# Macaron block on one core: group sums on GpSimd, ScalarE in program order in the attention, a written order for the first four tiles, and a base product behind the last gating

## The chip, the cores and the metric

The kernel runs on one core of one Trainium2 chip. The core has TensorE (PE in the profile; its weight loads are listed as PEld), VectorE (DVE), ScalarE (ACT), GpSimd (POOL) and SyncE (SP), which issues all the DMAs here. The metric is the device time of one launch in microseconds, lower is better. All data are 32-bit floats.

## The reference

Four sequences of 256 tokens, 512 features: 1024 tokens in all. The block is a feed-forward layer at half weight, attention, and the same feed-forward layer again:

```python
x = x + 0.5 * ffn(layernorm(x))
x = x + attn(layernorm(x))          # 32 query heads, 8 key/value heads of 128, rope,
                                    # softmax over a sliding window of 128 tokens, then @ wo
x = x + 0.5 * ffn(layernorm(x))

def ffn(xf):                        # 8 experts of rank 16, the best two of each token
    probs = softmax(xf @ W_router.T)
    w = top2(probs), divided by their sum
    h = einsum("td,erd->ter", xf, lora_A)
    return xf @ W_base.T + b_base + einsum("ter,eor,te->to", h, lora_B, w) * 2.0
```

The normalisations have no learned scale. Both feed-forward layers use the same weights, and each subtracts and divides per token before anything is multiplied.

## The kernel before

**Data.** The 1024 tokens are eight tiles `xt[0]` to `xt[7]` of 128 tokens (`x` in the profile), which stay in SBUF from the first load to the last store; tiles 0 to 3 are the first half, 4 to 7 the second. A half has two batches (sequences) of two tiles. The loads are issued on SP in this order: tiles 0 and 1, the narrow weights `ar_sb` (expert A matrices and router side by side, 136 columns), tiles 2 and 3, the base weights `wb_sb`, the bias, tiles 4 to 7, and then the attention weights.

**Feed-forward (`ffn`, L264 to 317)** is cut into steps named by a letter and a tile number, and strings such as "A0 M2 N2" give their order:
- M (`measure`, L198): on VectorE the statistics `st` (L200) and mean with variance `mv` (L202), on ScalarE the square root `sd` (L204).
- N (`norm`, L207): on VectorE the reciprocal `rs`, in the first layer (`f1`) also the shift `sh`; then the normalised tile `xc`, on ScalarE in `f1` and on VectorE in the others; four transposes on TensorE into one PSUM bank `pt` (L222) and a copy on ScalarE to `xn` (L223). M runs within N if it was not asked for before.
- A (`narrow`, L281): the product with the narrow weights, `pa` (L287), copied by ScalarE to `hl` (L291); GpSimd adds the bias to the tile (L292).
- R (`route`, L226 to 261): the top two of eight experts for all tiles of the step. That is a row of small VectorE operations, one exponential on ScalarE (L241), and the gating of `hl` by its shares on GpSimd (L261).
- B (`base`, L297): the base product `po` (L300), which stays open in its PSUM bank.
- G (`gated`, L302): the gated `hl` transposed on TensorE (L306) and copied to `ht` by ScalarE (L308).
- L (`leave`, L310): the last matmul into `po` (L312), then x + 0.5 po on VectorE (L313), then what follows for that tile: in `f1` the attention's normalisation of the tile before it, in the second layer (`f2`) the store.

**Attention.** The work is cut into units (half, group, batch): 2 halves, 8 key/value groups of 4 query heads, 2 batches, so 32 units with the half outermost; unit (1,7,1) is the last. For a unit:
- `scores` (L451): `sa` and `sb` on TensorE (L460, L473). VectorE adds the mask and takes the maxima `mx`. Queries of the first 128 tokens of a sequence attend within them; for the later ones two blocks of 64 keys are chosen.
- `exponentials` (L484): eight exponentials of 128x128 on ScalarE (L490), with their sums, and their reciprocal on VectorE (L494).
- `normalize` (L496): two products of 128x512 on GpSimd (L499).
- `transposes` (L503): eight transposes on TensorE. ScalarE copies one bank to `p0` (L508), VectorE masks the other twice into `p1` (L516, `p` in the profile).
- `values` (L522): two banks, `oa` (L527) and `ob` (L531). ScalarE copies each to `oT` (L528, L532). The copy of `ob` is what the output products wait for.
- `outputs` (L538): four groups of output products (`y`, L555), seven half-size products in place of eight by Strassen's scheme (in Winograd's form). The operand sums `oTs` are four GpSimd operations (`sums_a`, L114). The first group needs no sum, the second the second of them, the last two the others too. For a batch, the parts that belong to both tiles are gathered over the eight groups of a half in `z16` and `z75` (L564; at group 0 by a ScalarE copy, L560).
- `add_sums` (L571): after a half's last group, six additions a batch of `z` and `x` that finish the scheme, on VectorE (L581). For the first half it is queued in `late` behind the outputs of units (0,7,0) and (0,7,1), so it runs within the unit that follows each. For the second half both batches' sums run in unit (1,7,1), since group (1,7) of batch 1 takes plain products (`out_project`, L583 to 590) instead.

Between these run the projections of later groups: `keys` (`pp_k`, L351), `project_v` (`pv`, L444, copied by ScalarE at L448) and `queries` (L377, seven products again, with `u` and `v` as VectorE's temporary sums at L395, and `rope` at L333 to 346, whose last additions are GpSimd's). Their operand sums are `wqs` (L114) for the query weights, made two groups ahead in units with b = 1, and `wos` (L119) for the output weights, made in the group's own unit with b = 0, both on GpSimd.

**What sets the order.** The program is written in Tile, which schedules each engine's instructions by its own estimate of when they are ready, except for the engines named in `tc.manual_schedule`, which keep the order of the program. Before the attention, PE and DVE are in program order, but only for the first four tiles (L623). From the first unit on (L656), GpSimd alone is. Tile pools limit how far work may run ahead: PSUM has four banks with tag "mm" (products) and four with tag "s" (transposes, scores, `pa`); `wq`, `wqs`, `wos`, `ht` and `xs` have one buffer, `xc` three, `oT` four (it also holds `xn`).

The first layer's normalisation of four tiles and the first part of their products follow the string in L624, then the two halves' steps are interleaved (L626 to 631). The second layer for the first half is split by batches into eight pieces each ("N0", "N1 A0", ... "L1"), put into `loose` when its `add_sums` is queued, and taken from it in the last three units (L685 to 691): five pieces and one in unit (1,6,1), the same in (1,7,0), the last four in (1,7,1). The second layer for the second half follows the last unit, in the order of the list at L714, mixed with the last output projection (`None`).

Of the kernel before, what the change touches and what calls it, by code (L numbers as in the profile page):

```python
# [14 lines left out]
ALU = mybir.AluOpType  # L15
# [3 lines left out]
B, S, D = 4, 256, 512  # L19
T = B * S  # L20
NT = T // P
NH, NKV, HD = 32, 8, 128
G = NH // NKV
E, R = 8, 16
# [13 lines left out]
def macaron_kernel(  # L38
# [165 lines left out]
        nc.scalar.activation(std, mv[:, 1:2], AF.Sqrt, bias=eps)  # L204
        moments[tag, t] = mv, std

    def norm(t, xn, i, tag):  # L207
        if (tag, t) not in moments:
            measure(t, tag)
        mv, std = moments[tag, t]  # L210
        rstd = sb.tile([P, 1], F32, tag="rstd", bufs=4, name=f"rs_{tag}_{t}")
        nc.vector.reciprocal(rstd, std)
        xc = sb.tile([P, D], F32, tag="xc", bufs=3, name=f"xc_{tag}_{t}")
        if tag == "f1":
            shift = sb.tile([P, 1], F32, tag="shift", bufs=4, name=f"sh_{tag}_{t}")
            nc.vector.scalar_tensor_tensor(shift, mv[:, 0:1], -1.0, rstd, ALU.mult, ALU.mult)
            nc.scalar.activation(xc, xt[t], AF.Identity, bias=shift, scale=rstd)
        else:
            nc.vector.tensor_scalar(xc, xt[t], mv[:, 0:1], rstd, ALU.subtract, ALU.mult)
        pt = ps.tile([P, KC, P], F32, tag="s", bufs=4, name=f"pt_{tag}_{t}")  # L220
        for c in range(KC):
            nc.tensor.transpose(pt[:, c, :], xc[:, ts(c, P)], ident)  # L222
        nc.scalar.copy(xn[:, :, ts(i, P)], pt)  # L223
# [40 lines left out]
    def ffn(tiles, tag, then):  # L264
        n, t0 = len(tiles), tiles[0]
        xf, po, state = {}, {}, {}

        def x_of(i, c):
            return xf[i // 2][:, c, ts(i % 2, P)]

        def enter(i):
            if i % 2 == 0:
                xf[i // 2] = sb.tile(
                    [P, KC, 2 * P], F32, tag="oT", bufs=4, name=f"xn_{tag}_{tiles[i]}"
                )
            norm(tiles[i], xf[i // 2], i % 2, tag)

        def look(i):
            measure(tiles[i], tag)

        def narrow(i):  # L281
            t = tiles[i]
            if i == 0:
                state["hl"] = sb.tile([P, TPH, E * R + E], F32, tag="hl", name=f"hl_{tag}_{t0}")[:, :n, :]
            pa = score_bank(f"pa_{tag}_{t}")
            for c in range(KC):
                nc.tensor.matmul(  # L287
                    pa[:, : E * R + E], x_of(i, c), ar_sb[:, c, :],
                    start=(c == 0), stop=(c == KC - 1),
                )  # L290
            nc.scalar.copy(state["hl"][:, i, :], pa[:, : E * R + E])  # L291
            nc.gpsimd.tensor_tensor(xt[t], xt[t], half_bias, ALU.add)  # L292

        def shares():
            route(t0, n, state["hl"], tag)

        def base(i):  # L297
            po[i] = mm_bank(f"po_{tag}_{tiles[i]}")
            for c in range(KC):
                nc.tensor.matmul(po[i], x_of(i, c), wb_sb[:, c, :], start=(c == 0), stop=False)  # L300

        def gated():  # L302
            hl = state["hl"]
            pt = ps.tile([P, n, P], F32, tag="s", bufs=4, name=f"ph_{tag}_{t0}")
            for i in range(n):
                nc.tensor.transpose(pt[:, i, :], hl[:, i, : E * R], ident)  # L306
            state["ht"] = sb.tile([P, TPH, P], F32, tag="ht", bufs=1, name=f"ht_{tag}_{t0}")
            nc.scalar.copy(state["ht"][:, :n, :], pt)  # L308

        def leave(i):  # L310
            out, t = po.pop(i), tiles[i]
            nc.tensor.matmul(out, state["ht"][:, i, :], lb_sb, start=False, stop=True)  # L312
            nc.vector.scalar_tensor_tensor(xt[t], out, 0.5, xt[t], ALU.mult, ALU.add)  # L313
            then(t)

        steps = {"M": look, "N": enter, "A": narrow, "B": base, "L": leave, "R": shares, "G": gated}
        return lambda s: steps[s[0]](*(int(i) for i in s[1:]))


# [251 lines left out]
    def add_sums(h, b):  # L571
# [5 lines left out]
        for dst, other in (  # L577
            (z16[:, hi], z16[:, lo]), (x0, z16), (x0[:, hi], z75[:, hi]),
            (z75[:, lo], z16[:, hi]), (z75[:, hi], z75[:, lo]), (x1, z75),
        ):  # L580
            nc.vector.tensor_tensor(dst, dst, other, ALU.add)  # L581

    def out_project(h, g, b, i, oT):  # L583
        t = h * TPH + 2 * b + i
# [35 lines left out]


    halves = [ffn(tiles(h, 0, BPH), "f1", norm_later) for h in range(NHALF)]
    with tc.manual_schedule(engines={mybir.EngineType.PE, mybir.EngineType.DVE}):  # L623
        for step in "M0 M1 N0 N1 A0 M2 N2 A1 M3 N3 B0 A2 B1 A3".split():  # L624
            halves[0](step)
    for h, order in (  # L626
        (0, "R B2"), (1, "N0 N1"), (0, "B3 G"), (1, "A0"),
# [25 lines left out]
            queue.popleft()()  # L653

    last = units[-1]
    ctx.enter_context(tc.manual_schedule(engines={mybir.EngineType.Pool}))  # L656
    ahead = scores(*units[0])
    exponentials(*ahead)
    for u, (h, g, b) in enumerate(units):
# [34 lines left out]
        if left > 1:  # L694
            ahead = scores(*units[u + 1])
        else:
            f2 = [ffn(tiles(h, b, 1), "f2", store) for b in range(BPH)]
            f2[0]("N0")
            f2[0]("N1")
        oT = values(h, g, b, p0, p1)  # L700
        if left > 1:
            exponentials(*ahead)
# [9 lines left out]
                for n in ("N0", "N1 A0", "A1 R", "B0", "B1", "G", "L0", "L1")  # L712
            )
    for n, order in (  # L714
        (0, "A0 A1 R"), (None, 0), (0, "B0"), (None, 1), (1, "N0"), (0, "B1"), (1, "N1 A0 A1 R"),
        (0, "G L0 L1"), (1, "B0 B1 G L0 L1"),
    ):
        if n is None:
            out_project(*last, order, oT)
# [49 lines left out]
```

## Time and profile before

| | |
|---|---|
| time, median of 3 runs | 805.71 us (805.61 to 806.04) |
| time of the profiled execution | 806.56 us |
| its span, first to last instruction | 804.9 us |
| TensorE busy | 784.5 us, 97% |
| VectorE busy | 496.1 us, 62% |
| GpSimd busy | 462.0 us, 57% |
| ScalarE busy | 223.1 us, 28% |
| mean granted TensorE clock | 0.996 |
| DMA, mean | 61 GB/s |

The span is that of one profiled execution; the time is what the device took for a launch, so it is somewhat longer than its span. Rows of the profile name the engine, the line, the operation and the program's names with buffer numbers left out (`xc_f` is an `xc` of a feed-forward layer, `xc_a` one of the attention). The bracket behind a row is the time its engine stood idle before it, and what ended that. "Granted clock" is the share of full speed that TensorE was given. In the page's forty slices it is 1.0 or 0.9 in tenths nearly everywhere; one slice near the end shows 8. Times within the execution are counted from the start of the span: the first transposes start at 6.45 us, and the last matmul ends at 801.04.

### The profile page before, as it was taken

To read this page: it belongs to the slowest core of one execution; us is meant where nothing else is said; L and a number is where in the kernel's file an instruction comes from. 1 tells how busy PE (TensorE), PEld (TensorE's weight loads), DVE (VectorE), ACT (ScalarE), POOL (GpSimd) and SP (SyncE) were. 2 spreads that over 40 slices of the span, in tenths; PEclk is the share of its full clock that TensorE was granted. 3 is DMA by queue.
4 is the path that set the end of the run, shared out by engine and by line. 5 is a ranking of instruction groups with operands and counts; after the bars stand their busy time and mean duration, and the time that the engine had idled before them with its cause. 6 is when DMAs were issued, how large, how long until landed. Compare 5 with 4: busy or idle time off the path is not lost.

```text
span 804.9 us, 10161 instructions
## 1 busy us (share of the span) xinstructions
PE 784.5 (97%) x3524; PEld 604.4 (75%) x3524; DVE 496.1 (62%) x1222; ACT 223.1 (28%) x761; POOL 462.0 (57%) x520
## 2 busy tenths in 40 slices
PE   5999999999999999999999999999999999999897
PEld 4557878787878787887878787878787877867553
DVE  3458573738384847467689737483848474757553
ACT  5242333222222221314033332222222213123231
POOL 5412875766757474748475757666574747456221
PEclk9999999999999999999999999999999999999899
DMA  8400121212120203130221112121202020100001
GB/s 295 149 1 23 70 66 53 91 53 66 53 85 37 89 1 105 40 105 13 73 73 53 65 53 92 52 67 53 66 33 85 2 104 1 53 1 26 1 27 53
DMA packets 33556, 48.91 MB, mean 61 GB/s; under 512 B 1248, under 2 KB 14304, under 8 KB 33504
## 3 DMA queue, kind: packets, MB, share of 16 engines
q1 hardware_dynamic: 33504, 48.26, 17.8%
q8 instruction: 28, 0.46, 0.2%
q14 instruction: 24, 0.20, 0.1%
HBM read 46.15 MB, written 2.10 MB: 60 GB/s over the span
## 4 chain that ended last, share of the span: by engine, by line
PE 89%; DVE 6%; ACT 2%; POOL 1%; issue 1%; DMA 1%; SPq 0%; DVEq 0%; ACTq 0%
PE q L377 23%; PE y L555 22%; PE pp_k L351 7%; PE po_f L300 6%; PE pv L444 6%; PE ob L531 6%; PE sb L473 4%; PE sa L460 3%; PE oa L527 3%; PE pa_f L287 2%; PE po_f L312 2%; PE t L512 2%; PE t L507 2%; ACT pr L490 1%; PE y L587 1%; DVE z L581 1%
## 5 line engine op out<-in xcount | busy, mean ns | idle before, releaser
L344 POOL TENSOR_TENSOR qT<-ra_q,rb_q 128x256 f32<-128x256 f32 x64 | 46.6, 728 | 154.2 <-DVE rb_q L335 154.2
L555 PE MATMUL y<-wo,oT 128*128 128x256 f32 x368 | 95.7, 383 | 0.0
L335 DVE TENSOR_TENSOR rb_q<-q,sin_sb 64x512 f32<-64x512 f32 x128 | 88.1, 688 | 1.7
L114 POOL TENSOR_TENSOR oTs<-oT 128x256 f32<-128x256 f32 x62 | 45.6, 735 | 57.8 <-ACT oT L532 55.4
L555 PEld LDWEIGHTS y<-wo,oT 128*128 128x128 f32 x368 | 71.0, 193 | 10.0
L508 ACT COPY p<-t 128x512 f32<-128x512 f32 x32 | 18.8, 587 | 193.3 <-PE t L507 193.3
L564 DVE TENSOR_TENSOR z<-y,z 128x512 f32<-128x512 f32 x54 | 37.2, 689 | 54.4 <-PE y L555 54.4
L499 POOL TENSOR_TENSOR pr<-pr,sm 128x512 f32<-128x512 f32 x64 | 66.3, 1058 | 2.9 <-DVE sm L494 2.9
L555 PE MATMUL y<-wos,oTs 128*128 128x256 f32 x248 | 65.0, 385 | 0.9 <-POOL oTs L114 0.8
L490 ACT ACTIVATE pr<-pr,nm 128x128 f32<-128x128 f32 x128 | 50.0, 392 | 44.4 <-DVE nm L487 31.8
L444 PEld LDWEIGHTS pv<-wv,xa 128*128 128x128 f32 x256 | 48.6, 190 | 18.1 <-issue 12.9
L377 PE MATMUL q<-xa,wq 128*128 128x256 f32 x256 | 60.8, 379 | 0.0
L377 PE MATMUL q<-xs,wqs 128*128 128x256 f32 x256 | 60.6, 379 | 0.0
L377 PE MATMUL q<-xs,wq 128*128 128x256 f32 x256 | 60.5, 379 | 0.0
L531 PE MATMUL ob<-p,v 128*128 128x512 f32 x128 | 60.5, 593 | 0.0
L444 PE MATMUL pv<-wv,xa 128*128 128x256 f32 x256 | 60.0, 379 | 0.0
L351 PE MATMUL pp_k<-xa,wk 128*128 128x512 f32 x128 | 57.6, 593 | 0.3 <-DVE rb_q L335 0.3
L300 PE MATMUL po_f<-wb_sb,xn_f 128*128 128x512 f32 x128 | 57.7, 593 | 0.0
L564 DVE TENSOR_TENSOR x<-y,x 128x256 f32<-128x256 f32 (+1 forms) x62 | 33.8, 545 | 37.9 <-PE y L555 37.8
L555 PEld LDWEIGHTS y<-wos,oTs 128*128 128x128 f32 x248 | 47.3, 192 | 9.0 <-POOL oTs L114 2.5
L377 PEld LDWEIGHTS q<-xa,wq 128*128 128x128 f32 x256 | 48.5, 190 | 6.9 <-DVE mv_a L202 0.2
L377 PEld LDWEIGHTS q<-xs,wqs 128*128 128x128 f32 x256 | 48.6, 190 | 6.6
(138 smaller groups left out, 1546.8 us busy)
## 6 DMA issues: line engine op xcount, KB each, us to landing
wq<-in_wq_dram SPq DMA_DIRECT2D x16, 1024.0 KB, 5.5
wo<-in_wo_dram SPq DMA_DIRECT2D x16, 1024.0 KB, 5.0
wk<-in_wk_dram SPq DMA_DIRECT2D x16, 256.0 KB, 2.5
wv<-in_wv_dram SPq DMA_DIRECT2D x8, 512.0 KB, 3.5
x<-in_x_dram SPq DMA_DIRECT2D x8, 256.0 KB, 7.0
out_dram<-x SPq DMA_DIRECT2D x8, 256.0 KB, 2.0
wb_sb<-in_w_base_dram SPq DMA_DIRECT2D x1, 1024.0 KB, 8.0
ar_sb<-in_w_ar_dram SPq DMA_DIRECT2D x1, 272.0 KB, 5.2
```

The source lines that it names most:

```text
L114: nc.gpsimd.tensor_tensor(dst, p, q, op)
L300: nc.tensor.matmul(po[i], x_of(i, c), wb_sb[:, c, :], start=(c == 0), stop=False)
L335: nc.vector.tensor_tensor(twice(b[o : o + half, :]), twice(src[i : i + half, :]), angle(sin_sb[o : o + half, :]), ALU.mult,)
L344: nc.gpsimd.tensor_tensor(old_q, a[:, :, 0, :], b[:, :, 0, :], ALU.add)
L351: nc.tensor.matmul(pp, w[:, c, :], xa[h][:, c, :], start=(c == 0), stop=(c == KC - 1))
L377: nc.tensor.matmul(bank[:, ts(j, S)], w[:, c, ts(j, HD)], x[:, c, :], start=(new and j == 0 and c == 0), stop=(c == 1), skip_group_check=True,
L444: nc.tensor.matmul(pv[:, : 2 * HD], xa[h][:, c, ts(i, P)], weights["v", h, g][:, c, :], start=(c == 0), stop=(c == KC - 1),)
L490: nc.scalar.activation(pr[:, n, :], src, AF.Exp, bias=nm[:, n : n + 1], scale=scale, accum_out=sm[:, n : n + 1],)
L499: nc.gpsimd.tensor_tensor(w, w, sm[:, n : n + G].unsqueeze(2).to_broadcast([P, G, P]), ALU.mult)
L531: nc.tensor.matmul(po, v[:, 2 * b + n, cols], p1[n], start=(n == 0), stop=(n == 1))
L555: nc.tensor.matmul(py[:, ts(i, D // 2)], lhs[n - 1][:, c, :], weights["os", h, g][n - 1][:, c, :], start=(i == 0 and c == 0), stop=(c == 1 ...
L564: nc.vector.tensor_tensor(dst, py[:, : len(which) * D // 2], dst, ALU.add)
```

## The change

1. `norm` is split: `scale` makes `xc`, and `norm` transposes it. New steps are X (`scale` alone) and T (`norm` of a tile already scaled). The string for the first four tiles is new, and ScalarE is put in program order there too: tiles 0 and 1 are transposed and copied before tile 2 is scaled.
2. From the attention's first unit to the end, ScalarE keeps the program order, as GpSimd does.
3. The six additions of `add_sums` go from VectorE to GpSimd, where they stand in program order: in the units behind (0,7,0) and (0,7,1) between the normalisation (L499) and the weight sums, and in unit (1,7,1), for both batches, behind its normalisation.
4. In the last unit, "N0 N1" of the second layer's tiles 4 and 5 (in `f2[0]`) is placed behind `values` instead of ahead of it.
5. In the list for the last four tiles, the last base product B1 goes behind the last gating G.

```diff
--- before.py
+++ after.py
@@ -204,7 +204,7 @@
         nc.scalar.activation(std, mv[:, 1:2], AF.Sqrt, bias=eps)
         moments[tag, t] = mv, std
 
-    def norm(t, xn, i, tag):
+    def scale(t, tag):
         if (tag, t) not in moments:
             measure(t, tag)
         mv, std = moments[tag, t]
@@ -217,6 +217,12 @@
             nc.scalar.activation(xc, xt[t], AF.Identity, bias=shift, scale=rstd)
         else:
             nc.vector.tensor_scalar(xc, xt[t], mv[:, 0:1], rstd, ALU.subtract, ALU.mult)
+        moments[tag, t] = xc
+
+    def norm(t, xn, i, tag, scaled=False):
+        if not scaled:
+            scale(t, tag)
+        xc = moments[tag, t]
         pt = ps.tile([P, KC, P], F32, tag="s", bufs=4, name=f"pt_{tag}_{t}")
         for c in range(KC):
             nc.tensor.transpose(pt[:, c, :], xc[:, ts(c, P)], ident)
@@ -268,15 +274,21 @@
         def x_of(i, c):
             return xf[i // 2][:, c, ts(i % 2, P)]
 
-        def enter(i):
+        def enter(i, scaled=False):
             if i % 2 == 0:
                 xf[i // 2] = sb.tile(
                     [P, KC, 2 * P], F32, tag="oT", bufs=4, name=f"xn_{tag}_{tiles[i]}"
                 )
-            norm(tiles[i], xf[i // 2], i % 2, tag)
+            norm(tiles[i], xf[i // 2], i % 2, tag, scaled)
 
         def look(i):
             measure(tiles[i], tag)
+
+        def shape(i):
+            scale(tiles[i], tag)
+
+        def turn(i):
+            enter(i, scaled=True)
 
         def narrow(i):
             t = tiles[i]
@@ -313,7 +325,7 @@
             nc.vector.scalar_tensor_tensor(xt[t], out, 0.5, xt[t], ALU.mult, ALU.add)
             then(t)
 
-        steps = {"M": look, "N": enter, "A": narrow, "B": base, "L": leave, "R": shares, "G": gated}
+        steps = {"M": look, "X": shape, "T": turn, "N": enter, "A": narrow, "B": base, "L": leave, "R": shares, "G": gated}
         return lambda s: steps[s[0]](*(int(i) for i in s[1:]))
 
 
@@ -578,7 +590,7 @@
             (z16[:, hi], z16[:, lo]), (x0, z16), (x0[:, hi], z75[:, hi]),
             (z75[:, lo], z16[:, hi]), (z75[:, hi], z75[:, lo]), (x1, z75),
         ):
-            nc.vector.tensor_tensor(dst, dst, other, ALU.add)
+            nc.gpsimd.tensor_tensor(dst, dst, other, ALU.add)
 
     def out_project(h, g, b, i, oT):
         t = h * TPH + 2 * b + i
@@ -620,8 +632,10 @@
 
 
     halves = [ffn(tiles(h, 0, BPH), "f1", norm_later) for h in range(NHALF)]
-    with tc.manual_schedule(engines={mybir.EngineType.PE, mybir.EngineType.DVE}):
-        for step in "M0 M1 N0 N1 A0 M2 N2 A1 M3 N3 B0 A2 B1 A3".split():
+    with tc.manual_schedule(engines={
+        mybir.EngineType.PE, mybir.EngineType.DVE, mybir.EngineType.Activation
+    }):
+        for step in "M0 M1 X0 X1 T0 T1 M2 A0 X2 M3 A1 T2 X3 B0 T3 A2 B1 A3".split():
             halves[0](step)
     for h, order in (
         (0, "R B2"), (1, "N0 N1"), (0, "B3 G"), (1, "A0"),
@@ -653,7 +667,7 @@
             queue.popleft()()
 
     last = units[-1]
-    ctx.enter_context(tc.manual_schedule(engines={mybir.EngineType.Pool}))
+    ctx.enter_context(tc.manual_schedule(engines={mybir.EngineType.Pool, mybir.EngineType.Activation}))
     ahead = scores(*units[0])
     exponentials(*ahead)
     for u, (h, g, b) in enumerate(units):
@@ -695,8 +709,6 @@
             ahead = scores(*units[u + 1])
         else:
             f2 = [ffn(tiles(h, b, 1), "f2", store) for b in range(BPH)]
-            f2[0]("N0")
-            f2[0]("N1")
         oT = values(h, g, b, p0, p1)
         if left > 1:
             exponentials(*ahead)
@@ -712,8 +724,8 @@
                 for n in ("N0", "N1 A0", "A1 R", "B0", "B1", "G", "L0", "L1")
             )
     for n, order in (
-        (0, "A0 A1 R"), (None, 0), (0, "B0"), (None, 1), (1, "N0"), (0, "B1"), (1, "N1 A0 A1 R"),
-        (0, "G L0 L1"), (1, "B0 B1 G L0 L1"),
+        (0, "N0 N1 A0 A1 R"), (None, 0), (0, "B0"), (None, 1), (1, "N0"), (0, "B1"), (1, "N1 A0 A1 R"),
+        (0, "G L0 L1"), (1, "B0 G B1 L0 L1"),
     ):
         if n is None:
             out_project(*last, order, oT)
```

The scheduler answers to these. In the instruction lists of the changed program TensorE's first steps are the transposes of tiles 0 and 1, `pa` 0, `pa` 1, the transpose of tile 2, `po` 0, the transpose of tile 3, `pa` 2. VectorE has the statistics of tile 4 ahead of the `mv` of tile 3. The square roots of the first half's second layer, and what follows them, move from the time of the first sums to the end of the kernel. The order of the loads and stores on SP is as before.

## The prediction

> **What bounds the kernel now.** I read the page first (busy shares, the forty slices, the chain that ended last), then the waits, then the timeline in every place where TensorE idles.
>
> ```profile
> PE 784.5 (97%) x3524; PEld 604.4 (75%) x3524; DVE 496.1 (62%) x1222; ACT 223.1 (28%) x761; POOL 462.0 (57%) x520
> ...
> PE 89%; DVE 6%; ACT 2%; POOL 1%; issue 1%; DMA 1%; SPq 0%; DVEq 0%; ACTq 0%
> ```
>
> TensorE is busy 97% of the span and carries 89% of the chain. The change adds no matmul, so it can win only TensorE's idle time and any stretch at half clock; everything else is hidden while TensorE has a next matmul. Idle times of TensorE over 0.2 us in the timeline: 6.45 and 2.50 at the start; 0.42 at 381; 1.09 at 437; 0.28 at 448; 0.68 and 0.42 at 677 to 680; 3.21 at 749; 0.52 at 799; three of 0.24. The three large places:
>
> ```profile
> 10.27 0.57 ACT L223 COPY xn_f<-pt_f 128x512 f32<-128x512 f32 x1
> ...
> 10.89 2.18 PE L287 MATMUL pa_f<-ar_sb,xn_f 128*128 128x136 f32 x8 [2.50 <-ACT xn_f L223]
> ...
> 13.58 0.69 DVE L200 BATCH_NORM_STATS2 st_f<-x 128x6 f32<-128x512 f32 x1 [2.83 <-DMA x<-in_x_dram]
> ...
> 410.82 2.04 POOL L499 TENSOR_TENSOR pr<-pr,sm 128x512 f32<-128x512 f32 x2
> ...
> 412.82 1.45 POOL L114 TENSOR_TENSOR wqs<-wq 128x512 f32<-128x512 f32 x1
> ...
> 417.48 1.34 POOL L114 TENSOR_TENSOR wqs<-wq,wqs 128x512 f32<-128x512 f32 x1
> ...
> 421.58 0.72 POOL L114 TENSOR_TENSOR oTs<-oT 128x256 f32<-128x256 f32 x1 [2.76 <-ACT oT L532]
> ...
> 424.17 1.03 PE L555 MATMUL y<-wos,oTs 128*128 128x256 f32 x4
> ...
> 438.37 1.99 PE L377 MATMUL q<-xa,wqs 128*128 128x256 f32 x8 [1.09 <-DVE v L395]
> ...
> 740.09 1.65 DVE L581 TENSOR_TENSOR x<-x,z 128x512 f32<-128x512 f32 x1
> ...
> 748.98 0.40 ACT L490 ACTIVATE pr<-pr,nm 128x128 f32<-128x128 f32 x1 [5.78 <-DVE nm L486]
> ...
> 752.32 2.08 PE L555 MATMUL y<-wos,oT 128*128 128x256 f32 x4 [3.21 <-ACT oT L532]
> ```
>
> A row is start, duration, engine, line, tiles; the bracket is the idle time before it and what ended it. Front: the first transposed tile waits in ScalarE's queue until 10.27, behind tile 2. Middle: GpSimd has only 2.76 us of slack before the `oTs` sums, and TensorE takes them at 424.17 the moment they are there. Tail: VectorE's last group sums (L581) and the routing push the scores back, ScalarE starts its exponentials at 748.98, and `oT` comes behind five of them.
>
> ```profile
> core 0: us, PE busy (x) PEld busy (x) DVE busy (x) ACT busy (x) POOL busy (x), PEclk, DMA share, GB/s
> ...
> 754.90:758.30 3.40, 3.40 (x9) 2.68 (x9) 0.45 (x1) 0.00 (x0) 2.58 (x3) 0.50 0.00 0
> ```
>
> The table by stretch: TensorE is full, at granted clock 0.50, as from 751.5 on. The seven `y` groups take 9.26 us from 752.32, against 6.04 in the chain for other units: the wait at 749 costs 3.2 twice.
>
> **Front.** Splitting the normalisation in two adds no instruction; it moves them. ScalarE now copies tiles 0 and 1 (0.57 each) right after their transposes, at 7.5 and 8.5, so both `pa` products (2.18 each at the early half rate, as at 10.89) run from 8.4 to 12.7 at worst. But `hl` of tile 0 (to 10.9) stands ahead of `xc` of tile 2 (0.81, now to 11.8, was 10.06), and VectorE's order now puts the statistics of tile 4 ahead of `mv` of tile 3. Tile 4 lands at 13.58, and behind it wait `mv` 3 (to 14.5), its `sd` (14.8), `rs`, and `sh`, which ends near 15.85 behind a 1.24 us GpSimd op as the `sh` issued at 15.21 did; then ScalarE: `sd` 4, `xn` 2 (0.57), `xc` 3 to 17.06. So the transpose of tile 3 starts at 17.1 (was 14.90). What follows it, up to the third base product, is 0.44 + 0.93 + 3.43 + 0.93 = 5.7: it starts at 22.9 to 23.1, was 24.06. **-1.0**; bounds -2.0 and +0.3.
>
> **ScalarE in order in the attention.** The copy of `ob` goes ahead of the eight exponentials instead of behind three. At 378 it starts 0.75 earlier and the 0.42 wait at 381 goes: **-0.4**. At 677 `ob` itself ends at 677.2, the copy cannot be earlier, and 0.68 + 0.42 stay. Elsewhere a `pv` product stands between and covers it. The exponentials start up to 0.6 later; their normalisation is needed ten us later, after the queries, so that costs nothing.
>
> **Group sums on GpSimd, middle.** Per call four adds of 128x256 and two of 128x512. Nearest rows of the same engine: `oTs` 0.73 at a pitch of 0.805, `wqs` 1.27 at 1.35. GpSimd goes in program order, so the sums stand between L499 (to 412.82) and `wqs`. They wait twice for products: z16 412.85, x0 at 414.15 (its product is added until 414.08), x0's second half at 415.87, then 416.67, 417.47, 418.27 to 419.54. Behind them are four `wqs` (5.4) to 424.95 (before: 418.8), then `oTs`. Its third op, which the product of 424.17 needs, ends at 424.95 + 2 x 0.805 + 0.73 = 427.3. TensorE has meanwhile done the two groups that need no sum, to 424.0, and idles **3.3**. What comes back: VectorE no longer jams, so the 1.09 and 0.28 go, and about 0.3 of issue and of the `ob` wait. The second call ends at 436.3; the statistics that wait for it on VectorE hold `u` and `v` until 438.6, but TensorE wants `v` only at 440.3: 1.7 of cover, and past it TensorE would wait one for one. `wos` moves from 433.9 to 441.7, wanted after 451. SP's loads follow TensorE's reads and shift with it. Net **+1.5**; bounds +0.5 and +3.
>
> **Clock.** Does that 3.3 us idle halve the clock? The row says a wait of 3.21, with only 0.66 us of transposes around its start, did, for 6.8 us. The Trainium skill ("TensorE: Matmul & The Clock Gate", What's actually happening) says that the clock falls after at least one idle window of about 3.4 us, in windows that run freely. By the rule 3.3 does not fill a window, and the loss is 0; by the row it costs (6.8 - 1) / 2 = 2.9. The trace agrees with the window (6.8 is two of them) but fell after less than a whole one. The same page (Part 4) has transposes not counted as busy; then the idle stretch there was 748.33 to 752.32, 4.0, longer than mine. So I take no fall as likelier, 2.9 as the upper end.
>
> **Tail.** The normalisation of the first half's four tiles moves here from the middle: two more table loads on ScalarE net. The row has 1.28 (425.73), the skill ("ScalarE: Activation LUTs", What ACT_TABLE_LOAD costs) 2.66 with a drain; at 425.73 the square root follows at 427.03, so I use 1.28; by the rule two of these chains would be 1.4 later each, +2.8. Step by step:
> - 711.92: exponentials end 708.8, load and `sd` to 710.44, `xc` (0.55 alone, 1.6 beside GpSimd) by 711.9. The second `sd` queues behind `xn`, so the tiles go one by one: 0.7 idle instead of 0.48. +0.25.
> - 729: `oTs` is wanted one bias product (0.86) earlier than before: 0.6 idle (was 0.1), +0.4.
> - 736: again one by one, +0.2.
> - 740 to 750: without L581's 1.4 to 1.65 VectorE finishes the maxima at 749.2 or earlier, and the copy of `ob` no longer waits for exponentials: `ob` ends 749.1, copy to 749.85, `y` at 749.9, 0.7 idle before its sums, so `y` ends at 756.6. Before: 761.4. **-4.8** with the three lines above in it; the half clock is gone.
> - GpSimd's twelve sums now start after the last normalisation (756.45); x of tile 5 is complete at 762.3. VectorE's statistics wait for it, and behind them are two L313 and the masked `p`: the first `ob` goes at 765.55 instead of 763.8, **+1.75**, 0.3 more at `oa`.
> - The first `pt` of the last two tiles was under other work; now `xn` behind it is waited for, **+0.7** (and ScalarE's load before its `sd` ends at 769.25, covered by the out projection). The base product behind the last gating covers the copy that cost 0.52, **-0.5**: the gated shares are ready on GpSimd near 791.9 and wanted at 792.5.
> Sum -4.8 + 1.75 + 0.3 + 0.7 - 0.5: tail **-2.6**. Of the two loads, by the skill's figure, +2.8 more, which would eat it. Bounds -4.5 and +0.3.
>
> **Sum.** -1.0 - 0.4 + 1.5 - 2.6 = -2.5. The two ends added up, -6.4 and +3.2, do not come together; taken as independent they reach 2.4 below the forecast and 3.5 above (root of the squares), and half of each is what I allow the forecast itself. The profiled execution's own time is 806.56 (span 804.9, 1.66 around it), 0.85 above the median of 805.71. I take the difference off the median: **803.2**.
>
> **The rivals.**
> - *The half clock moves to the middle.* The idle stretch at 424 meets a free-running window badly: +2.9, 806.1, no change. For: the row at 749. Against: the rule and the missing transposes. 0.28.
> - *Slower: the sums are too dear for GpSimd.* One mechanism: they stand ahead of `oTs` in the middle and ahead of the statistics in the tail, so each us that six of them need over 5.5 costs about one at 424 and one at 765. With a longer stall the clock falls too (+2.9). It decides from 6.1 us for the six, since -2.5 + 2.9 + 2 x 0.6 = +1.6. For: L114 beside L581 took 1.45 and 1.61 for 1.27; at that rate 6.9 us, -2.5 + 2.9 + 2.8 = +3.2, 808.9. Against: after the move VectorE reads a PSUM operand in those stretches, beside which L114 stays at 1.27. 0.16.
> - *The front does not do what its order says*, tile 4 setting the pace as before: +1.0 on the forecast, 804.2; it lies in the forecast's own range, 802.0 to 804.9.
>
> **How the numbers follow.** Forecast 0.57 (the front rival 0.08 of it), half clock 0.27, dear sums 0.16. About 0.2% (1.6 us) can be told from no change: faster is below 804.1, slower above 807.3. Faster: the forecast without its front rival, 0.49. Same: that 0.08 and 0.22 of the half clock, 0.30. Slower: 0.05 of the half clock and the dear sums, 0.21. The range 801.6 to 807.8 leaves out 0.06 below and 0.14 above.
>
> **What would show it.** Right: `pa` from 8.4 and the third transpose near 17; one TensorE wait of 3.3 on POOL `oTs` near 423, none on `v`; no wait of 3.2 on ACT `oT` and clock 1.00 near 750; a wait of 1.7 on DVE `p` near 763. Wrong: clock 0.50 after the middle wait; sums over 0.85 and 1.4 each; a tail that ends within 1 us of the old one.

## The result, and the profile after

The changed kernel takes 803.88 us (median of 20 executions, 802.21 to 806.15) against 805.87 us before (20 executions); the ratio is 0.9975, 95% interval 0.9968 to 0.9983. That is 2.0 us faster, where 2.5 was forecast (803.2). The profiled execution took 804.62 us, with a span of 802.9.

The first lines are from the page of the changed kernel: busy shares, and the chain that ended last.

```profile
PE 783.9 (98%) x3524; PEld 603.7 (75%) x3524; DVE 477.6 (59%) x1198; ACT 225.7 (28%) x763; POOL 481.8 (60%) x544
...
PE 92%; POOL 3%; DVE 1%; DMA 1%; ACT 1%; issue 1%; SPq 0%; ACTq 0%; DVEq 0%; POOLq 0%
```

About 19 us of work went from VectorE to GpSimd, and GpSimd, which had 1% of the chain, now has 3%. The timeline of the changed kernel says where (start, duration, engine, line, tiles; in the bracket the idle time before, and what ended it):

```profile
8.21 3.99 PE L299 MATMUL pa_f<-ar_sb,xn_f 128*128 128x136 f32 x16
...
22.06 3.60 PE L312 MATMUL po_f<-wb_sb,xn_f 128*128 128x512 f32 x8
...
29.81 1.41 PE L318 MATMUL ph_f<-ident,hl_f 128*128 128x128 f32 x4
...
425.24 2.02 PE L567 MATMUL y<-wos,oTs 128*128 128x256 f32 x4 [2.93 <-POOL oTs L114]
...
751.09 1.13 PE L567 MATMUL y<-wos,oT 128*128 128x256 f32 x4 [0.46 <-ACT oT L544]
...
764.41 1.12 PE L539 MATMUL oa<-p,v 128*128 128x512 f32 x2 [0.29 <-ACT p L520]
766.02 1.98 PE L543 MATMUL ob<-p,v 128*128 128x512 f32 x4 [0.48 <-DVE p L528]
...
772.60 1.98 PE L312 MATMUL po_f<-wb_sb,xn_f 128*128 128x512 f32 x4 [0.73 <-ACT xn_f L229]
```

The 2.50 us wait in front of `pa` is gone. The waits on v and rb at 437 and 448 are gone, and one of 2.93 us on GpSimd's `oTs` stands ahead of them. The 3.21 us wait in the tail is 0.46. The table by stretch shows what follows the wait of 2.93 (PEclk, the granted clock, is the third value from the end):

```profile
core 0: us, PE busy (x) PEld busy (x) DVE busy (x) ACT busy (x) POOL busy (x), PEclk, DMA share, GB/s
422.00:424.00 2.00, 0.30 (x2) 0.00 (x0) 0.20 (x1) 0.66 (x4) 1.92 (x3) 1.00 0.00 0
424.00:426.00 2.00, 0.77 (x2) 0.68 (x3) 0.00 (x0) 0.00 (x0) 1.84 (x4) 0.83 0.00 0
426.00:428.00 2.00, 2.00 (x6) 1.55 (x6) 0.69 (x1) 0.00 (x0) 1.98 (x2) 0.50 0.00 0
428.00:430.00 2.00, 2.00 (x9) 1.69 (x8) 0.18 (x1) 0.00 (x0) 0.72 (x1) 0.82 0.00 0
```

The half clock of the tail has moved to the middle, and here it lasts about 3.4 us, not 6.8. The same TensorE instruction in both profiled executions, us from the start:

| instruction | before | after | difference |
|---|---|---|---|
| third base product | 24.06 | 22.06 | -2.00 |
| fourth transpose of the first gating | 32.13 | 30.89 | -1.24 |
| `y` on `oTs`, behind the old wait at 381 | 381.56 | 379.79 | -1.77 |
| `ob` ahead of the middle's wait | 420.28 | 418.26 | -2.02 |
| `y` on `oTs`, behind the middle | 468.65 | 469.37 | +0.72 |
| first `y` behind the 0.68 us wait at 677 | 677.88 | 678.50 | +0.62 |
| first `y` behind the last exponentials | 752.32 | 751.09 | -1.23 |
| end of the last matmul | 801.04 | 799.06 | -1.98 |

The middle costs 2.7, of which 1.8 is the half clock (the difference grows from 1.07 to 2.86 between 425.24 and 428.75). The tail brings 2.6.

Of the 20 executions 7 have a mean granted clock of 0.999 or 1.000, and their median is 802.5; the other 13 have 0.998 or less, and theirs is 804.3. The kernel before has 0.998 or less in all of the 35 executions that ran beside the last experiments. 27 of them have 0.998, like the changed kernel's profiled execution with its one stretch of 3.4 us at half clock; only 8 have 0.996, like the profiled execution of before with 6.8 us. So the profile of before shows about twice the half clock of most executions.

### The profile page after: what moved, and what is told of

Read it like the earlier page. It is cut to its first block, busy times and chain, and to the rows that moved or that the text cites. A ratio compares the mean times of both kernels' runs of the same rounds, so it can differ in the third digit from the quotient of the medians.

```text
span 802.9 us, 10176 instructions
## 1 busy us (share of the span) xinstructions
PE 783.9 (98%) x3524; PEld 603.7 (75%) x3524; DVE 477.6 (59%) x1198; ACT 225.7 (28%) x763; POOL 481.8 (60%) x544
## 4 chain that ended last, share of the span: by engine, by line
PE 92%; POOL 3%; DVE 1%; DMA 1%; ACT 1%; issue 1%; SPq 0%; ACTq 0%; DVEq 0%; POOLq 0%
PE q L389 24%; PE y L567 22%; PE pp_k L363 7%; PE pv L456 7%; PE ob L543 7%; PE po_f L312 6%; PE sb L485 5%; PE sa L472 3%; PE oa L539 3%; PE t L519 2%; PE t L524 2%; PE pa_f L299 2%; PE po_f L324 1%; DMA x<-in_x_dram 1%; PE y L599 1%; PE pt_f L228 1%
```

## The experiments

"before" in each is the kernel before on the same chip, at 805.6 to 805.7 us. In the code excerpts engine names are shortened (`PE` for `mybir.EngineType.PE`), and `...` stands for lines left out.

### The new front alone

The split of `norm` into `scale` and `norm` is in it too.

```
-    with tc.manual_schedule(engines={PE, DVE}):
-        for step in "M0 M1 N0 N1 A0 M2 N2 A1 M3 N3 B0 A2 B1 A3".split():
+    with tc.manual_schedule(engines={PE, DVE, Activation}):
+        for step in "M0 M1 X0 X1 T0 T1 M2 A0 X2 M3 A1 T2 X3 B0 T3 A2 B1 A3".split():
```

> The kernel before with the new order of the first four tiles alone. Theory: the order gains what the two traces show up to the end of the first layer. The third base product starts 2.0 us earlier (22.06 against 24.06), and at the first gating 0.8 of that is given back, because its four transposes then wait one by one for GpSimd; 1.2 us stay. Expected 804.6 to 804.8 against 805.8. Rival one: the later stages take it all back, since they are paced by waits of their own (381, 437, 749 us): within 0.3 us of the kernel before. Rival two: nothing is given back but in this one profile: 803.8.

Measured: 803.66 us (11 executions), ratio 0.9978, interval 0.9969 to 0.9986, so 1.1 to 2.5 us faster. In its trace the fourth gating transpose starts 1.5 us earlier, and everything behind it keeps that until the half clock in the tail, so the first rival is out. (Its half clock lasts 3.41 us and not 6.83; from there on the trace is 2.5 us ahead.) The median lies below the expected 804.6 to 804.8 and nearer to the second rival, but the interval holds the 1.2 to 1.5 us of the traces as well; what the median has beyond them is not explained. What gives back a part is seen in the two traces around 30 us: the gating of `hl` on GpSimd ended at 31.81 before, just when TensorE came (31.80); after, it ends at 30.83, and TensorE is there at 29.81. TensorE gained 2.0, the routing that it waits for only 1.0.

### The group sums alone

```
-            nc.vector.tensor_tensor(dst, dst, other, ALU.add)
+            nc.gpsimd.tensor_tensor(dst, dst, other, ALU.add)
```

> The kernel before with the group sums on GpSimd alone. Theory: VectorE is free before the last exponentials, so the tail gains by the sums and not by ScalarE's order: the 3.21 us wait on the copy of ob at 749 shrinks to under 1.5 us, its half clock goes, and the tail gains 2 to 3 us; in the middle GpSimd's sums cost a wait of about 3 us on the oTs sums near 424 and take away the waits on v and rb: 0.7 to 2.5 us lost, by whether the clock falls. Net -2 to +0.5: 803.8 to 806.3. Rival: it is ScalarE's order that pulls the copy of ob ahead of the exponentials, and without it the copy still stands behind some of them: the wait at 749 stays over 2.5 us with its half clock, and the kernel is slower than before by 0.7 to 2.5 us, 806.5 to 808.3.

Measured: 806.49 us (9 executions), ratio 1.0017 (1.0008 to 1.0026), 0.9 us slower, at the edge of what either theory gave. The middle has its wait (2.96), and the tail is half of each theory: the wait at 749 is 1.72 us, and no half clock follows it. ScalarE's timeline of this kernel shows why it is not shorter:

```profile
749.35 0.40 ACT L490 ACTIVATE pr<-pr,nm 128x128 f32<-128x128 f32 x1 [6.12 <-DVE nm L486]
...
752.06 0.57 ACT L532 COPY oT<-ob 128x512 f32<-128x512 f32 x1
```

Six exponentials, the one shown among them, and the copy of `oa` stand ahead of the copy of `ob`. And a new place appears near 766, where the normalisation put ahead of the values waits for GpSimd's sums (0.77 and 0.90 us on `xc_f`); the granted clock in this execution is 0.91 from 760 to 780. The profiled execution, 808.35 us, was the slowest of the nine.

### The first half's sums back on VectorE

```
-            nc.gpsimd.tensor_tensor(dst, dst, other, ALU.add)
+            (nc.gpsimd if h else nc.vector).tensor_tensor(dst, dst, other, ALU.add)
```

> The changed kernel with the first half's twelve group sums (the middle) back on VectorE, the second half's (the tail) on GpSimd. Theory: the sums on GpSimd pay in the tail and cost in the middle, by their place ahead of the weight sums and oTs: the 2.93 us wait goes, 1.1 and 0.3 us come back on v and rb, and the half clock of the middle, which takes 1.8 us in some executions, goes with the long wait. Expected 801.3 to 802.6, and a clock of 1.00 from 400 to 450 us. Rival: the middle is even, what GpSimd costs VectorE costs too, and the spread of the times is not from this wait: 803.3 to 804.3, with the same spread of some 3 us.

Measured: 799.66 us (5 executions, 799.20 to 800.65), ratio 0.9934 (0.9922 to 0.9946): 5.9 us faster than before and 1.6 better than the theory's best. All at clock 1.000. The wait of 2.93 is gone, and the waits on v and rb do not come back although VectorE has the sums again. The kernel before, VectorE around `u` and `v`:

```profile
427.62 2.07 DVE L219 TENSOR_SCALAR xc_f<-x,mv_f,rs_f 128x512 f32<-128x512 f32 x2
...
436.53 0.67 DVE L395 TENSOR_TENSOR u<-q,p1c 128x512 f32<-128x512 f32 x1
437.12 0.54 DVE L219 TENSOR_SCALAR xc_f<-x,mv_f,rs_f 128x512 f32<-128x512 f32 x1
437.57 0.17 DVE L202 BATCH_NORM_AGGREGATE mv_f<-st_f 128x2 f32<-128x6 f32 x1
437.66 0.66 DVE L395 TENSOR_TENSOR v<-q,u 128x512 f32<-128x512 f32 x1
```

And this kernel:

```profile
433.39 0.67 DVE L407 TENSOR_TENSOR u<-q,p1c 128x512 f32<-128x512 f32 x1
433.98 0.17 DVE L202 BATCH_NORM_AGGREGATE mv_f<-st_f 128x2 f32<-128x6 f32 x1
434.17 0.69 DVE L407 TENSOR_TENSOR v<-q,u 128x512 f32<-128x512 f32 x1
```

Three `xc_f` and their reciprocals stood ahead of `v`, beside the sums. They are not here: their square roots are on ScalarE, which now keeps program order and has them at the end. The sums alone do not make `v` late; with the `xc_f` among them they did.

### The first half's sums on GpSimd, but behind `oTs`

```
             late.extend(outputs(h, g, b, oT))
+            run(sums, len(sums))
...
-            late.append(lambda h=h, b=b: add_sums(h, b))
+            sums.append(lambda h=h, b=b: add_sums(h, b))
```

> The changed kernel with the first half's twelve group sums on GpSimd as well, but each six of them behind the oTs sums of the unit in which they ran, ahead of the next normalisation. Theory: only their place costs. Neither the 2.93 us wait nor the waits on v and rb are there, and no half clock: 803.9 - 2.9 - 0.9 (the mean of a half clock in half of the executions) = 799.6 to 800.6. Rival: GpSimd has no room for 6.6 us more at either place; the normalisation, the wos sums or the statistics on VectorE, which wait for the sums, come late instead, and a wait of 2 to 3 us turns up between 425 and 455: 802.5 to 804.5.

Measured: 806.61 us (14 executions), ratio 1.0009 (0.9999 to 1.0019), 2.7 us worse than the changed kernel. The theory fell; the rival names the effect, though not that it is dearer. VectorE of this kernel, then TensorE:

```profile
428.34 0.69 DVE L200 BATCH_NORM_STATS2 st_f<-x 128x6 f32<-128x512 f32 x1 [1.92 <-POOL x L593]
428.95 0.67 DVE L576 TENSOR_TENSOR z<-y,z 128x512 f32<-128x512 f32 x1
...
454.20 0.69 DVE L200 BATCH_NORM_STATS2 st_f<-x 128x6 f32<-128x512 f32 x1 [5.18 <-POOL x L593]
454.81 0.67 DVE L345 TENSOR_TENSOR ra_k<-pp_k,cos_sb 128x512 f32<-128x512 f32 x1
455.50 1.39 DVE L347 TENSOR_TENSOR rb_k<-pp_k,sin_sb 64x512 f32<-64x512 f32 x2
```

```profile
429.68 1.99 PE L389 MATMUL q<-xs,wqs 128*128 128x256 f32 x8 [1.40 <-DVE z L576]
...
457.04 1.97 PE L567 MATMUL y<-wo,oT 128*128 128x256 f32 x4 [3.34 <-DVE rb_k L347]
```

The scheduler leaves the second layer's statistics early in VectorE's queue. They wait for the sums, and the PSUM reads behind them (`z`, `rb_k`) wait too, until TensorE has no free bank. It is not GpSimd that lacks room but VectorE that stands waiting for it.

### ScalarE's order alone

```
-    ctx.enter_context(tc.manual_schedule(engines={Pool}))
+    ctx.enter_context(tc.manual_schedule(engines={Pool, Activation}))
```

> The kernel before with ScalarE in program order from the attention's first unit on, and nothing else. Theory now: it is this part that takes the waits on v and rb out of the middle, since the square roots of the second layer's first half stay in their place near the end, and with them the reciprocals and the xc (L219) that stood in VectorE's queue ahead of v; and it is this part that takes the copy of ob ahead of the exponentials at 749. Expected: no wait at 381, 437 and 448 (-2.4 with what lies around them), a wait under 1.2 us instead of 3.21 at 749 and no half clock (-3.5 to -5), +0.9 for tiles normalised one by one: 799.5 to 801.0, at clock 1.00. Rival, as the prediction had it: ScalarE's order is worth 0.4 us at 381; v waits as long as VectorE has the sums, and the wait at 749 keeps 2 us: 804.0 to 805.4.

Measured: 805.89 us (13 executions), ratio 1.0005 (0.9997 to 1.0013): no difference. Half of the theory holds: there is no wait at 381, 437 or 448, TensorE gains 2.0 us from 381 to 468, and the wait at 749 is 0.46. But the profile has a wait of 2.82 us on `xc_f` at 737, and one of 1.65 at 768, which take it back. The first is of the kind shown for the next kernel:

```profile
739.60 0.66 PE L222 MATMUL pt_f<-ident,xc_f 128*128 128x128 f32 x4 [2.82 <-DVE xc_f L219]
```

### All sums on VectorE, the rest of the change as it is

```
-            nc.gpsimd.tensor_tensor(dst, dst, other, ALU.add)
+            nc.vector.tensor_tensor(dst, dst, other, ALU.add)
```

> The changed kernel with all 24 group sums back on VectorE, so the other four parts of the change together. Theory now: in the tail too the sums gain nothing by GpSimd once ScalarE is in order; what VectorE saves before 750 is given back when the statistics and ob wait for GpSimd after 757: within 0.6 us of the kernel with only the tail's sums on GpSimd (799.7), so 799.1 to 800.3, at clock 1.00. Rival, as the prediction had it: the last sums on VectorE push the maxima and the exponentials back, the wait at 749 is over 1.5 us again, and the clock falls behind it: 801.5 to 804.

Measured: 803.87 us (21 executions), ratio 0.9974 (0.9967 to 0.9980). The changed kernel has 803.88: on the whole the move of the sums to GpSimd is worth nothing. As the rival had it the sums do cost in the tail, but not at 749 (0.46 there too). TensorE, ScalarE and VectorE of this kernel:

```profile
739.39 1.12 PE L228 MATMUL pt_f<-ident,xc_f 128*128 128x128 f32 x4 [2.84 <-DVE xc_f L219]
```

```profile
733.93 0.59 ACT L229 COPY xn_f<-pt_f 128x512 f32<-128x512 f32 x1 [3.84 <-PE pt_f L228]
734.42 0.30 ACT L204 ACTIVATE sd_f<-mv_f,eps 128x1 f32<-128x1 f32 x1
```

```profile
736.44 0.15 DVE L212 RECIPROCAL rs_f<-sd_f 128x1 f32<-128x1 f32 x1
736.55 1.39 DVE L593 TENSOR_TENSOR z<-z 128x256 f32<-128x256 f32 x1
737.86 1.48 DVE L219 TENSOR_SCALAR xc_f<-x,mv_f,rs_f 128x512 f32<-128x512 f32 x1
```

In program order the square root of a step's second tile comes behind the copy of its first `xn`, at 734.42; the reciprocal and `xc` that wait for it stand behind L593 sums in VectorE's queue. TensorE waits 2.84 us, and loses clock in 13 of 21 executions.

### One of the middle sums back on VectorE

```
+            eng = nc.vector if (h, b) == (0, 0) and dst is x1 else nc.gpsimd
-            nc.gpsimd.tensor_tensor(dst, dst, other, ALU.add)
+            eng.tensor_tensor(dst, dst, other, ALU.add)
```

> The changed kernel with one of the twelve middle sums (the last of the first six, 128x512) back on VectorE, so that GpSimd comes 1.3 us earlier to the oTs sums. Both theories: the wait at 424 is 1.5 to 1.7 us instead of 2.93. Theory (the clock falls only when a wait nearly fills a window of 3.41 us, which runs freely): no run loses clock, all lie within 1 us, and the median is that of the changed kernel's runs at clock 1.00 (802.4) less 1.3: 800.8 to 801.6. Rival (the spread over 2 us has another cause, such as the loads): the clock falls in some runs as before, between 0.995 and 0.998, and the median is 802.3 to 803.

Measured: 801.17 us (5 executions, 800.64 to 802.67), ratio 0.9950 (0.9938 to 0.9963), all at clock 1.000. The wait is even shorter than expected (0.94 at 422, after 0.73 on `p` at 417), since TensorE reaches it later. The median is as the theory says, not as the rival.

### The wait made longer

```
+        if (h, b) == (0, 0):
+            nc.gpsimd.tensor_tensor(z16, z16, z75, ALU.add)
```

> The changed kernel with one more GpSimd addition of 128x512 behind the first six middle sums; it adds z75 into z16, which nothing reads any more. Both theories: the wait at 424 is 2.93 + 1.35 = 4.3 us. Theory (the clock falls when the idle stretch fills enough of a window of 3.41 us that runs freely, so the longer the surer): every run loses clock, none is at 1.00, and the median is 802.4 (the changed kernel at full clock) + 1.3 + 1.7 to 3.4 = 805.4 to 807.1. Rival (the fall has to do with the run, not with the wait's length): still about a third of the runs at clock 1.00, and the median is 803.9 + 1.3 = 805.2.

Measured: 806.07 us (13 executions, 805.52 to 807.03), ratio 1.0006 (0.9998 to 1.0014). All 13 lose clock (0.995 to 0.998). TensorE of this kernel:

```profile
426.89 1.56 PE L567 MATMUL y<-wos,oTs 128*128 128x256 f32 x4 [4.16 <-POOL oTs L114]
```

The theory's median and count hold, the rival's (805.2, a third at 1.00) do not.

### Both tiles of a step measured first, with the tail's sums on GpSimd and with all on VectorE

```
-    for n in ("N0", "N1 A0", ...
+    for n in ("M0 M1 N0", "N1 A0", ...
...
-    (0, "N0 N1 A0 A1 R"), ... (1, "N0"), ...
+    (0, "M0 M1 N0 N1 A0 A1 R"), ... (1, "M0 M1 N0"), ...
```

With the first half's sums on VectorE, the second's on GpSimd:

> A version that the runs so far point to: the changed kernel with the middle's sums on VectorE, and in the second layer the statistics and square roots of both tiles of a step named ahead of the first normalisation, so that the second square root does not stand behind the copy of xn in ScalarE's order. Theory: the three waits of 0.67, 0.67 and 1.0 us on xn (709, 734, 768 us) shrink to 0.24 or less, the rest stays: 799.7 less 1.2 to 1.7 = 798.0 to 798.5. Rival: the two tiles' transposes stand together and pa waits for the second xn instead, as in the kernel before (0.24 each), and the last pair is held up by its later sum anyway: 798.9 to 799.7.

Measured: 799.89 us (5 executions, 799.52 to 800.32), ratio 0.9928 (0.9914 to 0.9942). Against 799.66 without it that is no difference, the rival's case: 0.98 us on `xc_f` takes the place of 0.68 at 709, 0.24 that of 0.68 at 735, and 0.83 that of 1.01 at 768.

With all sums on VectorE:

> All 24 group sums on VectorE, ScalarE in order, front and tail order as changed, and the statistics and square roots of both tiles of a step named ahead of the first normalisation. Theory: the 2.84 us wait at 737 with the sums on VectorE comes from two orders that meet: the second square root stands behind the copy of the first xn on ScalarE, and its xc behind three more sums on VectorE. With the square roots together the second xc moves ahead of most sums, the wait shrinks to under 1.0 us, the clock stays at 1.00, and all sums on VectorE are as good as the tail's on GpSimd: 799.5 to 800.7. Rival: VectorE has no room for the last six sums in any order; the wait only moves to the routing or the maxima (2 us or more between 737 and 752, clock below 1.00 in half of the runs): 802 to 804.

Measured: 799.97 us (5 executions, 799.87 to 800.88), ratio 0.9931 (0.9919 to 0.9943), 3.9 us better than without it. TensorE of this kernel, where 2.84 us were:

```profile
734.80 0.66 PE L228 MATMUL pt_f<-ident,xc_f 128*128 128x128 f32 x4 [1.21 <-DVE xc_f L219]
```

The wait is 0.2 longer than the theory allowed, and the rest as it says. So, with both tiles measured first, VectorE has room for every sum, and this version, the one above and the one with the middle's sums on VectorE are alike, all 5.7 to 6.0 us faster than before.

### The second layer's normalisation ahead of the last values

```
             f2 = [ffn(tiles(h, b, 1), "f2", store) for b in range(BPH)]
+            f2[0]("N0")
+            f2[0]("N1")
...
-        (0, "N0 N1 A0 A1 R"), (None, 0),
+        (0, "A0 A1 R"), (None, 0),
```

> The changed kernel with the first two normalisations of the last four tiles put ahead of the last unit's values again. Theory: in ScalarE's order the square roots and the copies of xn then stand ahead of the copies of oa and ob, and the last output projection waits for normalised tiles that wait for GpSimd's sums: 1.5 to 2.5 us more between 763 and 775, 805.4 to 806.4 (with the half clocks of the middle as they are). Rival: the order is of no account, since TensorE has the same work to put between: 803.5 to 804.3.

Measured: 807.11 us (14 executions), ratio 1.0017 (1.0006 to 1.0028), 3.2 us worse than the changed kernel: more than expected. ScalarE of this kernel:

```profile
763.72 1.28 ACT L204 ACT_TABLE_LOAD   x1
765.02 0.29 ACT L204 ACTIVATE sd_f<-mv_f,eps 128x1 f32<-128x1 f32 x1
...
770.73 0.58 ACT L229 COPY xn_f<-pt_f 128x512 f32<-128x512 f32 x1 [2.13 <-PE pt_f L228]
771.21 0.59 ACT L540 COPY oT<-oa 128x512 f32<-128x512 f32 x1
```

The copy of `oa` stands behind both `xn`, TensorE waits 2.25 us, and 9 of 14 executions have a clock of 0.995 or less. In its profiled execution (clock 0.998) TensorE ends 0.8 us later than in the changed kernel's. At equal clock this kernel is 1.7 to 2.0 us slower than the changed one (medians at 0.998: 805.9 against 804.3, of 3 and 6 executions; at 1.000: 804.4 against 802.4, of 2 and 5), which is what the theory gave. The rest of the 3.2 us is clock, which the theory left out: the nine executions at 0.995 or less took 806.7 to 809.4 us.

### ScalarE free, all else as changed

```
-    ctx.enter_context(tc.manual_schedule(engines={Pool, Activation}))
+    ctx.enter_context(tc.manual_schedule(engines={Pool}))
```

> The changed kernel with ScalarE free again from the first unit on. Theory: with GpSimd's sums, ScalarE's order is worth the copy of ob at 750 (a wait of 1.7 us against 0.46, as in the kernel with the sums alone) and 0.4 us at 381, less 0.9 for tiles normalised one by one: 0.6 to 1.2 us, so 804.5 to 805.1; the waits on v and rb stay away, since the sums are off VectorE. Rival: the square roots and xc of the first half go back to the middle and v waits again (1 us or more near 438): 805.3 to 806.5.

Measured: 805.47 us (13 executions), ratio 1.0001 (0.9992 to 1.0009), so ScalarE's order is worth 1.6 us within the change, above the theory's 0.6 to 1.2. The waits are 0.42 at 381, 1.75 at 750 and 1.45 on `p` at 767; there is none on v, though three `xc_f` are ahead of it again. With the sums away VectorE has room for them, so the rival's cause is out, though the time lies in the rival's range.

## Why the prediction was right, and where that was luck

The predicted time was 0.7 us off. By its own steps:

- *Front, -1.0.* Its order of events is in the trace, and tile 4 does set the pace: in the eleven traces with the new front the fourth gating transpose starts 17.7 to 17.8 us after the statistics of tile 4 do. Those start when the tile has landed, at 11.79 to 13.59, so the transpose comes at 29.47 to 31.43; in the three traces with the old front it comes at 31.42 to 32.13. The third base product came at 22.06 instead of 22.9 to 23.1, and 0.5 of that is a load that landed at 13.08 instead of the assumed 13.58: where it landed at 13.59 (ScalarE free), the product came at 22.58. The prediction ended its path there. The next thing that ends late is the routing of the first gating, and 0.8 of the 2.0 us go there. The net, 1.2 in the trace (0.7 at the same landing, 31.43 against 32.13), is near the -1.0 by errors of opposite sign and a load that came early.
- *ScalarE in order, -0.4.* Right in its place at 381, but the term was mis-sized, because a second effect was put down to the wrong part. The waits on v and rb go with ScalarE's order alone, since the normalised tiles leave VectorE's queue in the middle; the prediction had read `v` as queued behind the sums and credited the sums' move with it. To take away either is enough: they are also gone with the sums alone moved.
- *Middle, +1.5.* A wait of 3.3 was worked out and 2.93 came; without the clock the stretch costs 1.0. The mechanism and place are right. What it was set against is not: with ScalarE in order, the sums on VectorE cost the middle nothing, so that the move by itself costs 4.2 us in the median (803.88 against 799.66), and 2.9 at full clock (802.5).
- *Clock, 0.* Wrong in 13 of 20 executions, right in 7. Its price was taken as 2.9, from a profile with 6.83 us at half clock, and is 1.8, with 3.41. The forecast 803.2 lies between the medians of the two groups, 802.5 and 804.3; that is luck.
- *Tail, -2.6.* The trace has -2.6. The wait at 749 fell to 0.46 (0.7 foreseen), xn costs 0.73 (0.7), and the 0.52 behind the last gating is gone. In the sum, `y` is done 4.1 us earlier and not 4.8, and the 1.75 on `p` and 0.3 at `oa` are 0.77 together. With 0.73 and -0.52 that makes -3.1; the other 0.5 is that a stop costs more than its idle time, some 0.26 us: full-speed products of 512 columns overlap (0.59 long, 0.43 apart), and the first one behind a stop takes 0.70. There are two stops more than before. The -4.8 was also taken off the median, though it holds 3.2 us of half clock from a profile with twice the half clock of most executions; in the trace of the front alone, with the same 3.21 us wait, the half clock cost 1.1 us less. Executions with a mean clock of 0.998 on both sides differ by only 1.2 us (medians 805.5 and 804.3); the 2.0 us of the result needs the 7 executions of the changed kernel that lost nothing. The table loads took 1.28 us, as the row said, and the next instruction, where it was ready, starts 0.01 us later. The kernels with one part each show that this gain is no property of the sums or of ScalarE's order: the first alone leaves 1.72 us at 749, the second makes 2.82 at 737; only both together clear the tail, and the measurement first of both tiles does it without GpSimd.
- *Dear sums*, the rival for slower: out. The sums ran at 0.73 and 1.26 us, at the pitch that was assumed.

Two slips of the prediction bear on nothing else: in the tail six exponentials, not five, stand ahead of the copy of `ob`, and the half clock has 0.28 in one place and 0.27 in the other.

So the forecast sum is right to a quarter, and its division among the parts is not: the front alone has the whole 2.0 us of the median (803.66, against 803.88 with all parts), and the other parts together are near nothing, because the middle gives back what the tail gains. Not foreseen at all was that 4 us could be had by leaving the middle's sums where they were.

## What to carry to other kernels

Moving work to a less busy engine does not free the path where that engine, too, is in order: look at what stands behind it there, and at what a third engine, waiting for it, holds up in its own queue. Before a wait is put down to the operation named, list everything that stands ahead in that queue, and ask which of it is only there because a scheduler hoisted it; fixing the order of one engine can move work on another. Test parts in pairs, not only alone: here two parts gave +0.3 and +0.9 us alone, and one place of the second spoiled 4 us of what both together gained.

## What was not expected of the hardware

The granted clock can fall after a wait shorter than the one in the prediction, and by chance. The longest wait of TensorE behind the first layer (from each profile), and the executions with a mean clock of 0.998 or less:

| kernel | longest wait, us | executions that lost clock |
|---|---|---|
| four versions without a long wait | 0.94 to 1.21 | 0 of 20 |
| ScalarE's order alone | 2.82 | 5 of 13 |
| all sums on VectorE | 2.84 | 13 of 21 |
| the changed kernel | 2.93 | 13 of 20 |
| ScalarE free | 2.94 | 9 of 13 |
| normalisation ahead of the values | 2.94, and 2.25 at 768 | 12 of 14 |
| the group sums alone | 2.96 | 7 of 9 |
| front alone | 3.21 | 9 of 11 |
| the kernel before | 3.21 | 35 of 35 |
| middle sums behind `oTs` | 3.34 | 9 of 14 |
| the wait made longer | 4.16 | 13 of 13 |

The traces show more than the count. From there to the last products the recorded clock stays at 1.00 or 0.50 for multiples of 3.413 us only (737.28 is 216 of them, 413.01 is 121), and their edges lie differently in each trace. Divide each trace into stretches of that length, and look at the stretch ahead of each fall:

| trace, stretch | TensorE without an instruction in it, us | clock in the next one |
|---|---|---|
| the changed kernel, 421.91 to 425.32 | 2.93 | 0.50 |
| the kernel before, 748.09 to 751.50 | 2.51 | 0.50 |
| front alone, 748.91 to 752.33 | 2.00 | 0.50 |
| the group sums alone, 765.41 to 768.83 | 1.67 | 0.50 |
| ScalarE's order alone, 767.66 to 771.07 | 1.65 | 1.00 |
| front alone, 745.50 to 748.91 | 1.37 | 1.00 |

All eleven falls, in ten of the traces, follow a stretch with 1.67 to 3.34 us without an instruction, and no stretch with 1.65 or less is followed by one. (The ends of matmuls are modelled, so the limit is rough.) A stretch that was about half idle was enough, and it need not be one wait: in the kernel with the group sums alone it holds waits of 0.77 and 0.90.

The Trainium skill ("TensorE: Matmul & The Clock Gate", What's actually happening) has the clock fall after at least one idle window of about 3.4 us, in windows that run freely. The length and the free running agree with the traces. That a whole idle window is needed does not: half of one was enough. The counts are not all explained by that. An estimate from these traces, 1.66 us of a 3.413 us window on a free grid, gives 0.97 for the 3.21 us of the kernel before, which fell in 35 of 35, but 0.89 for 2.93 us, and 13 of 20 are 0.65. The waits of the executions that were not profiled are not known, so this stays open. The same page (Part 4) has transposes not counted as busy. The traces speak against it here: 2.58 us without a product (ScalarE's order alone, 767.66) and 2.39 us (ScalarE free, 764.54), each with 0.9 us of transposes, kept the full clock, and 2.00 us without a product and without a transpose (the front alone, 748.91) did not.
